# A cross-attention block on one core: the written-out front of the program in a new order, with 137 instead of 140 empty TensorE instructions

## The chip, the core and the metric

The kernel runs on one core of one Trainium2 chip. The core has five engines that work through queues of their own and wait for each other by semaphores: TensorE (PE in the profile, its weight loads PEld), VectorE (DVE), ScalarE (ACT), GpSimd (POOL) and SyncE (SP; SPq are the DMA issues of its queue). The metric is the device time of one execution in microseconds (us). Lower is better.

## The reference

A transformer block with cross-attention: 128 batches of 128 tokens, 256 features (D), 16 heads of 16 features, a feed-forward width of 1024, all float32. `query` is `x`, `key` and `values` are both `ctx`; `mask` is 0, so a token attends only to earlier ones and the first row of the attention is zero.

```python
q = (query @ Wq + bq).reshape(b, s, N_HEADS, D_K).transpose(0, 2, 1, 3)
k = (key @ Wk + bk).reshape(b, s, N_HEADS, D_K).transpose(0, 2, 1, 3)
v = (values @ Wv + bv).reshape(b, s, N_HEADS, D_K).transpose(0, 2, 1, 3)
scores = jnp.einsum('bhqd,bhkd->bhqk', q, k) / jnp.sqrt(jnp.float32(D_K))
...
allowed = j < i + mask
scores = jnp.where(allowed, scores, NEG_INF)
attn = jax.nn.softmax(scores, axis=-1)
if mask == 0:
    attn = attn.at[:, :, 0, :].set(0.0)
ctx = jnp.einsum('bhqk,bhkd->bhqd', attn, v)
...
attn_out = ctx @ Wo + bo
x = layer_norm(query + attn_out, ln1_g, ln1_b)
ffn = jax.nn.relu(x @ W1 + b1) @ W2 + b2
out = layer_norm(x + ffn, ln2_g, ln2_b)
```

## The kernel before

**Tiling.** Two batches are one pair `p`, 0 to 63. A pair goes through these stages: its tokens are loaded in 32x32 blocks (`load`, L92) and turned (`tokens`); queries, keys and values are projected; `scores` and `scores_both` (L440) multiply queries by keys into eight banks of PSUM; the mask, the maximum, the exponential and the sum follow; the attention is turned, `weigh` (L586) multiplies it by the values, `context` takes the product out of its bank, `attention_out` applies Wo, `attention_sum` adds the tokens; then come the first layer norm, the hidden layer (`hidden`), the second product (`second`) and the second norm. The scores of a pair fall into a high half (queries 64 to 127 of each batch, 128 keys a row) and a low half (queries 0 to 63, which need 64 keys).

**Order.** The kernel is written with a manual schedule: on each of the five engines the instructions stand in the order in which the Python statements issue them, and no scheduler moves any. So the place of a statement in the code is the place of all its instructions, on every engine it uses, the DMA issues included. Pairs 0 to 6 and steps 7 and 8 are written out one statement at a time; this is the front. A step `p` is not one pair: it has the scores of pair p, the weighing of pair p-2, the hidden layer of pair p-3, the second product of pair p-4 and the second norm of pair p-6. In steps 7 and 8 each statement is `do(key, p)`, with `key` from the table `OPS`. From step 9 on the loop `for p in range(9, 61): step(p)` takes its keys from one string, `ORDER`. Steps 61 to 63 are written out again. `empty(n)` puts n empty instructions into TensorE's queue.

**Softmax, two ways.** For pairs 0 to 4, `maximum` takes the maximum of a part on VectorE (L475) and subtracts it on GpSimd (L476), `exponential` is one wide ScalarE instruction, and `sums` takes the row sums and reciprocals on VectorE (L499) and scales the part on GpSimd (L500). From pair 5 on, `exponential_by_head` (L937) does one head at a time on ScalarE, with the maximum as bias and the sum as a by-product, and the reciprocals are applied later, when `context` reads the product. High-half heads are read from the PSUM banks, four heads to a bank, and free them; low-half heads are read from `sm` in SBUF, where `mask` put them. In steps 7 and up `eh0` to `eh7` are two high heads each, `el0` to `el7` two low heads each.

**Turning the attention.** Pairs 0 and 1 are turned on TensorE (`turn_on_pe`). From pair 2 on, `turn` transposes 32x32 blocks on VectorE from `sm` into the one buffer `turned` (L533), in three parts, and `bring` moves the blocks across partitions with 16 DMAs from `turned` to `brought` (L552), most of them issued by SyncE. `weigh` reads `brought`. Both buffers exist once, so pair p+1 can be turned only when the 16 transfers of pair p have read `turned`, and be brought only when pair p has been weighed.

**Mixed weights.** From step 7 on a 2x2 block product is done with seven products instead of eight (class `Seven`; `v1` to `v4`, `q1` to `q4`, `k1` to `k4`, `o1` to `o4`), and the same in the hidden layers of later pairs. For this GpSimd makes sums of weight blocks once (`combine_weights`, L1105 to L1108, four instructions for each of Wq, Wk, Wv and Wo; `combine_w1`, `combine_w2`) and sums of data blocks for every pair (`combine_x`, `combine_c`; `xc`, `cc`, `oc`, `hs`, `xs` in the steps). In a step, `v1`, `v2`, `v3`, `v4` write to one bank in turn, and `vk0`, `vk1`, `vk2`, `vr` are the ScalarE copies (`vr` is L1278) that empty it between them.

**Other names.** `add_bo` (L295, GpSimd) adds the output bias to the tokens of a pair. `residual1` (L721 and the line behind it, GpSimd) makes the input of the second sum. `deviation` and `shift` (GpSimd) make the scales of a norm. `load_ahead(p)` issues the block loads of later tokens: for an even p those of `x` of pairs p+4 and p+5, for an odd p those of `ctx` of pairs p+3 and p+4. `load_tokens(g)` loads the plain tokens of pairs 2g and 2g+1, `store(p)` writes a result. `tokens_ahead` is the same as `load_tokens` for the steps.

## Time and profile before

| | |
|---|---|
| time of three runs | 1468.98, 1472.11, 1474.38 us, median 1472.11 |
| the profiled execution | 1469.98 us, of which 1468.2 are its span |
| granted TensorE clock, mean over the span | 0.997 |
| HBM | 55.06 MB read, 18.09 MB written |
| front, up to the first weighing of step 9 | 184.8 us |
| loop, steps 9 to 60 | 52 rounds of about 22.0 us |

The profile counts an engine as busy while an instruction of it runs; register, branch, semaphore and DMA-issuing instructions do not count. In the timeline a row is a group of instructions of one line: start, length, engine, line, operation, output and input tile, count, and in brackets the idle time ahead of it and what ended it. The windows give for each stretch the busy time of each engine, the number of its instructions in brackets, the granted TensorE clock (1.00 is full), the busy share of the DMA engines and the GB/s that they moved. Times are counted from the start of the span. All names of pairs are cut from the tiles in the profile, so that the pair is known from the time and the order.

### The profile page before, as it was taken

What the parts mean: (1) busy time and instruction counts of PE and PEld (TensorE: products, weight loads), DVE (VectorE), ACT (ScalarE), POOL (GpSimd) and SP (SyncE); (2) the same over time, 40 slices, a digit from 0 to 9 for tenths busy, and PEclk for the clock granted to TensorE, in tenths of its full rate; (3) what the DMA queues carried; (4) which work ended last, traced back from release to release, by engine and by line L of the source; (5) the groups of instructions that cost most, each with busy time, mean ns of one, the idle gap of its engine ahead of it and who ended that gap; (6) DMA issues with size and microseconds to landing.
All of it is one profiled execution on the core that took longest, in us unless ns stands there. A gap on an engine that the chain in (4) does not pass through costs nothing.

```text
span 1468.2 us, 62017 instructions
## 1 busy us (share of the span) xinstructions
PE 1447.0 (99%) x20713; PEld 1391.6 (95%) x20713; DVE 1371.9 (93%) x3175; ACT 1303.4 (89%) x5559; POOL 1271.2 (87%) x1872
## 2 busy tenths in 40 slices
PE   8999899999999999999999999999999999999998
PEld 7778799999999999999999999999999999999988
DVE  6987999999999999999999999999999999999767
ACT  5659899999999999999999999999999999999743
POOL 5986898988988988988988998998998998998966
PEclk9999999999999999999999999999999999999999
DMA  8274766766766766766766766766766776774541
GB/s 208 63 143 102 179 154 156 162 157 156 161 160 153 162 158 153 163 160 153 160 158 157 159 158 158 160 158 156 163 157 153 163 161 149 164 158 116 140 103 51
DMA packets 367881, 220.34 MB, mean 150 GB/s; under 512 B 280032, under 2 KB 335584, under 8 KB 367584
## 3 DMA queue, kind: packets, MB, share of 16 engines
q1 hardware_dynamic: 365296, 214.27, 63.8%
q8 instruction: 187, 3.06, 1.0%
q10 hardware_dynamic: 2288, 2.11, 0.7%
q14 instruction: 110, 0.90, 0.2%
HBM read 55.06 MB, written 18.09 MB: 50 GB/s over the span
## 4 chain that ended last, share of the span: by engine, by line
PE 92%; DVE 4%; POOL 1%; DMA 1%; ACT 1%; issue 1%; SPq 0%; DVEq 0%; ACTq 0%; POOLq 0%
PE banks L1153 48%; PE banks L1364 24%; PE banks L440 6%; PE banks L596 4%; PE banks L586 2%; PE banks L300 2%; PE banks L875 2%; PE banks L977 1%; PE banks L635 1%; PE banks L356 1%; DVE sm L464 1%; ACT sm L937 1%; DVE turned L533 1%; PE banks L1050 0%; PE banks L1412 0%
## 5 line engine op out<-in xcount | busy, mean ns | idle before, releaser
L937 ACT ACTIVATE sm<-banks,nmx 128x128 f32<-128x128 f32 x944 | 340.8, 396 | 17.9 <-DVE nmx L1568 14.7
L937 ACT ACTIVATE sm<-sm,nmx 128x64 f32<-128x64 f32 x944 | 325.2, 384 | 1.5 <-DVE nmx L926 1.5
L937 ACT ACTIVATION_READ_ACCUMULATOR sm<-banks,nmx 128x1 f32 x944 | 222.8, 236 | 0.0
L937 ACT ACTIVATION_READ_ACCUMULATOR sm<-sm,nmx 128x1 f32 x944 | 221.8, 235 | 0.0
L533 DVE STREAM_TRANSPOSE turned<-sm 128x1024 f32<-128x1024 f32 x186 | 217.0, 1214 | 3.3 <-DMA brought<-turned 1.8
L1153 PE MATMUL banks<-wt,hS 128*128 128x128 f32 x1344 | 177.7, 275 | 0.0
L1364 PE MATMUL banks<-xS,w1t 128*128 128x128 f32 x1344 | 177.2, 275 | 0.0
L1153 PEld LDWEIGHTS banks<-wt,hS 128*128 128x128 f32 x1344 | 163.6, 192 | 0.1
L1364 PEld LDWEIGHTS banks<-xS,w1t 128*128 128x128 f32 x1344 | 163.4, 192 | 0.0
L1568 DVE TENSOR_REDUCE nmx<-banks 128x4 f32<-128x512 f32 x224 | 152.3, 680 | 1.9
L1557 POOL TENSOR_TENSOR hS<-hT 128x512 f32<-128x512 f32 x116 | 148.2, 1279 | 3.7 <-ACT hT L882 2.4
L1364 PE MATMUL banks<-brought,w 128*128 128x128 f32 x896 | 118.2, 275 | 0.0
L1153 PE MATMUL banks<-w,hT 128*128 128x128 f32 x896 | 109.8, 275 | 0.0
L1364 PEld LDWEIGHTS banks<-brought,w 128*128 128x128 f32 x896 | 109.0, 192 | 0.0
L1618 POOL TENSOR_TENSOR x1b<-x,g_r 128x512 f32<-128x512 f32 x56 | 72.4, 1293 | 39.4 <-ACT x L709 39.4
L1153 PEld LDWEIGHTS banks<-w,hT 128*128 128x128 f32 x896 | 104.8, 192 | 0.1
L440 PE MATMUL banks<-kT,qT 32*64 32x128 f32 (+1 forms) x3840 | 98.3, 331 | 1.8 <-ACT vz L1278 1.5
L1393 ACT ACTIVATE hT<-hT,b1e_c 128x256 f32<-128x256 f32 x224 | 95.7, 510 | 1.2 <-DVE hT L1389 1.1
L1562 DVE TENSOR_TENSOR banks<-banks,neg 128x256 f32<-128x256 f32 x224 | 93.3, 417 | 0.0
L440 PEld LDWEIGHTS banks<-kT,qT 32*64 32x64 f32 x3840 | 79.4, 131 | 12.6 <-ACT vz L1278 1.9
L709 ACT ACTIVATE x<-t,nb,sd 128x256 f32<-128x256 f32 x126 | 68.4, 593 | 19.7 <-POOL nb L732 12.9
L1219 ACT ACTIVATE kr<-banks,b_c 128x128 f32<-128x128 f32 x224 | 83.7, 411 | 1.7 <-PE banks L1153 1.7
(324 smaller groups left out, 4821.5 us busy)
## 6 DMA issues: line engine op xcount, KB each, us to landing
brought<-turned SPq DMA_DIRECT2D x936, 128.0 KB, 2.4
out_dram<-t SPq DMA_DIRECT2D x63, 256.0 KB, 4.0
xb<-in_x_dram SPq DMA_DIRECT2D x124, 128.0 KB, 3.2
cb<-in_ctx_dram SPq DMA_DIRECT2D x124, 128.0 KB, 3.2
x<-in_x_dram SPq DMA_DIRECT2D x56, 256.0 KB, 2.8
kT<-kr SPq DMA_DIRECT2D x112, 128.0 KB, 2.2
brought<-turned SPq DMA_DIRECT2D x40, 96.0 KB, 2.4
w<-in_L_xattn_W_dram SPq DMA_DIRECT2D x2, 1024.0 KB, 7.4
```

What stands on the lines that cost most here:

```text
L440: nc.tensor.matmul(st["sps", hi][r][s * HP : (s + 1) * HP, m * 2 * n : (m + 1) * 2 * n].rearrange("p (e j) -> p e j", e=2), st["qT"][strip ...
L533: nc.vector.transpose(turned[:, :, at : at + 256].rearrange("p j (n a) -> p n j a", a=32), states[p]["sm", hi].rearrange("p h j -> p (h j) ...
L709: nc.scalar.activation(x1[:, s], t1[:, s], AF.Identity, bias=st["nb", 1][:, s], scale=sd[:, s])
L937: nc.scalar.activation(sm[:, h, :], src, AF.Exp, bias=nmx[:, h : h + 1], scale=1.0, **({"accum_out": st["su"][:, at : at + 1]} if summed e ...
L1153: nc.tensor.matmul(out, left(k) if self.depth > 1 else left, right(k) if self.depth > 1 else right, start=(n == 1 and k == 0), stop=(k == ...
L1219: nc.scalar.activation(self.k[:, m, s * P : (s + 1) * P], src, AF.Identity, bias=bk_c[:, m : m + 1], scale=1.0,)
L1364: nc.tensor.matmul(ps[:, i * P : (i + 1) * P].rearrange("p (n a) -> p n a", a=32), left(i), right, start=(n in (1, 2, 5) and i == 0), stop ...
L1393: nc.scalar.activation(self.hT[:, f, at], self.hT[:, f, at] if src is None else src, AF.Relu, bias=b1e_c[:, f : f + 1], scale=1.0,)
L1557: engine.tensor_tensor(c[:, n], left, right, how)
L1562: nc.vector.tensor_tensor(ps[:, :, HP:], ps[:, :, HP:], neg[:, 1, None, :].to_broadcast([P, 4, HP]), ALU.add)
L1568: nc.vector.tensor_reduce(states[p]["nmx", 1][:, 4 * b : 4 * b + 4], banks[:, b].rearrange("p (n j) -> p n j", j=P), AX.X, ALU.max, negate ...
L1618: nc.gpsimd.tensor_tensor(st["x1b"], st["x1b"] if n else st["x1"], (be1b_r if n else g1_r)[:, None, :].to_broadcast([P, 2, D]), ALU.add if ...
```

## The change

The statements between `states[3]["x1T"] = x1_view(3)` and the loop stand in a new order. The same statements are called with the same arguments; the counts of instructions on VectorE, ScalarE, GpSimd and SyncE stay as they were, and TensorE has 137 empty instructions between the products of steps 7 and 8 where it had 140 (27 groups of five and one of two, for 28 groups of five). Nothing ahead of the front and nothing from step 9 on is touched. Two calls that were split by others now stand together (`second(0, 0)` with `second(0, 1)`, and the same for pair 1), and the halves of `bring(2, ...)` are issued in the other order.

The diff, cut to where statements move past many others. First the start and pairs 0 to 2, with `combine_weights` of all four weights:

```diff
     states[3]["x1T"] = x1_view(3)
     tokens(2, "x")
+    combine_weights(wv, wvt)
+    combine_weights(wo, wot)
     scores(0, 1)
     mask(0, 1, A)
...
+    hidden(0, range(0, 2), None, (2, 3, 4, 0))
+    hidden(0, range(2, 4), None, (2, 3, 4, 0))
+    combine_weights(wq, wqt)
+    turn_on_pe(1, 1, range(3, 4))
...
+    sums(2, 0, ALL)
+    combine_weights(wk, wkt)
+    add_bo(3)
+    turn(2, 1, 1)
+    context(1)
+    project_keys(3)
+    turn(2, 1, 0)
+    attention_out(1)
+    load_ahead(2)
+    turn(2, 0, 0)
     tokens(4, "c")
...
+    load_ahead(3)
     copy_keys(3)
```

Pairs 2 to 4, with the loads, the transfers of pair 2 and `add_bo(4)`:

```diff
-    bring(2, nc.sync, EVERY[:8])
-    context(1)
-    residual1(0)
-    scores(3, 1)
-    mask(3, 1, B)
-    bring(2, nc.scalar, EVERY[8:])
...
+    residual1(0)
+    bring(2, nc.scalar, EVERY[8:])
     hidden(0, range(6, 8), None, (2, 3, 4, 0))
...
+    exponential(3, 1, TWO)
+    bring(2, nc.sync, EVERY[:8])
+    weigh(2)
...
+    load_ahead(4)
+    nc.gpsimd.tensor_tensor(b1e_c, b1e_c, b1_c, ALU.add)
+    load_ahead(5)
...
-    load_ahead(2)
-    load_ahead(4)
...
-    add_bo(4)
-    tokens(6, "x")
-    combine_w1()
...
-    load_ahead(3)
-    copy_keys(5)
-    copy_queries(5)
-    load_ahead(5)
...
+    load_tokens(2)
     attention_out(3)
...
-    combine_weights(wk, wkt)
...
-    combine_weights(wo, wot)
...
+    store(0)
+    bring_all(5, EVERY[0:4])
...
-    combine_weights(wq, wqt)
...
+    add_bo(4)
     attention_sum(4)
...
-    combine_weights(wv, wvt)
```

Step 7 up to the scores of step 8. Before, in its last part:

```diff
-    do("v4", 7)
-    do("stats1", 7)
-    do("means", 7)
-    do("turn1", 7)
-    do("k4", 7)
-    do("q4", 7)
-    do("kr", 7)
-    do("eh0", 7)
-    do("qr", 7)
-    do("weigh", 8)
-    do("eh1", 7)
...
-    do("context", 8)
-    do("oc0", 8)
-    do("el4", 7)
-    do("el3", 7)
-    do("ks2", 7)
-    do("el7", 7)
-    do("turn2", 7)
-    do("vr", 7)
-    do("scores", 8)
-    do("maskA0", 8)
```

And in the change:

```diff
+    do("eh1", 7)
+    do("tokc", 7)
+    do("vr", 7)
+    do("br1", 7)
+    do("weigh", 8)
+    do("turn1", 7)
+    do("ks", 7)
+    do("hs0", 7)
     do("hs1", 7)
+    do("eh0", 7)
+    do("means", 7)
+    do("eh2", 7)
+    do("el3", 7)
     do("hs2", 7)
...
+    do("context", 8)
+    do("el1", 7)
+    do("xs2", 7)
+    do("hs3", 7)
+    do("ks2", 7)
+    do("scores", 8)
     do("turn0", 7)
+    do("add3", 8)
+    do("max3", 8)
+    do("el2", 7)
+    do("el6", 7)
```

And the empty instructions, where the products of steps 7 and 8 stand between each other:

```diff
+    do("w1", 7)
+    do("w5", 7)
+    empty(2)
     do("q1", 8)
     empty(5)
+    do("v2", 8)
+    empty(5)
...
     do("o1", 8)
     empty(5)
-    do("w1", 7)
...
-    do("w5", 7)
-    empty(5)
-    do("add1", 8)
```

More of the change, by code (lines that the diff above doesn't have):

```diff
@@ L2151, in tile_cross_attention_block @@
     exponential_by_head(6, 0, range(8, 12), True)
[L2152 to L2155 removed]
     second_half(2, 1)
+    turn_x1_blocks(4)
+    do("weigh", 7)
+    do("context", 7)
     exponential_by_head(6, 0, range(0, 4), True)
[L2158 to L2160 removed]
+    copy_keys(7)
+    do("res0", 7)
+    do("oc2", 7)
+    hidden(3, range(2, 4), None, (2, 3, 4, 6))
+    load_ahead(6)
+    turn(6, 1, 1)
```

733 lines of the change are left out of this document (356 added, 377 removed).

## The prediction

> **What bounds the kernel now.** I read the page first, then the chain of waits, then the busy time by stage, and then the timelines of single engines at the stage borders.
>
> ```profile
> span 1468.2 us, 62017 instructions
> PE 1447.0 (99%) x20713; PEld 1391.6 (95%) x20713; DVE 1371.9 (93%) x3175; ACT 1303.4 (89%) x5559; POOL 1271.2 (87%) x1872
> ```
>
> TensorE (PE) is nearly always busy, so time is saved only where it waits. The chain of waits shows the loop behind the front (columns: start, length, what):
>
> ```profile
> 188.10 8.24 PE banks L1153 x72
> ...
> 210.06 8.24 PE banks L1153 x72
> ...
> 232.03 8.23 PE banks L1153 x72
> ```
>
> The same piece returns after 21.96 and 21.97 us. The loop `step(9)` to `step(60)` is the same code in both kernels, so its 52 rounds cost the same, and the change acts on the 184.8 us ahead of it. This table cuts the front at its stage borders; the last row is one loop round (columns: stretch, its length, busy us of PE, weight loads, VectorE, ScalarE, GpSimd, then clock and DMA).
>
> ```profile
> 23.00:62.20 39.20, 38.68 (x527) 30.89 (x526) 35.91 (x54) 32.57 (x65) 36.70 (x26) 1.00 0.34 77
> 62.20:84.20 22.00, 21.61 (x218) 18.45 (x217) 21.27 (x36) 10.61 (x19) 20.81 (x19) 1.00 0.75 162
> 84.20:104.50 20.30, 20.30 (x240) 17.41 (x239) 17.43 (x24) 9.73 (x21) 18.07 (x13) 1.00 0.71 150
> 104.50:125.50 21.00, 19.58 (x237) 15.60 (x235) 17.35 (x32) 18.61 (x85) 9.78 (x19) 1.00 0.43 97
> 125.50:146.80 21.30, 21.30 (x246) 17.98 (x246) 16.66 (x29) 19.77 (x86) 16.25 (x26) 1.00 0.57 119
> 146.80:163.00 16.20, 11.43 (x218) 9.74 (x217) 13.77 (x35) 14.54 (x79) 11.45 (x20) 1.00 0.67 159
> 163.00:184.80 21.80, 21.19 (x235) 20.55 (x235) 21.30 (x50) 19.52 (x88) 19.78 (x32) 1.00 0.81 193
> 206.80:228.80 22.00, 22.00 (x331) 21.56 (x329) 21.34 (x52) 20.88 (x93) 19.68 (x30) 1.00 0.70 158
> ```
>
> PE's idle time from 23 us to the loop is 0.52 + 0.39 + 0 + 1.42 + 0 + 4.77 + 0.61 = 7.7 us. That is the ceiling for any new order of the same PE work, apart from short waits inside busy rows. It is 0.52% of the time, and 0.5% (7.4 us) is about what a measurement of this kernel can tell from no change. So "faster" needs nearly all of it. From 20 to 82 us GpSimd is as full as PE (36.70 of 39.20, 20.81 of 22.00): whatever is added to its queue there delays the softmax of the first pairs.
>
> **The change, part by part.** No instruction is added or removed except three empty ones, so the cost lies in which wait ends last. Two places carry the sum.
>
> First place: GpSimd. These are its rows around the scaling of pair 2 (L500, `sm_2`), before; L476 `sm_3` is the next pair's subtraction:
>
> ```order
> L500 TENSOR_TENSOR sm_2_705<-sm_2_705,rs1_2_8_862 128x1024
> L500 TENSOR_TENSOR sm_2_705<-sm_2_705,rs1_2_0_873 128x1024
> L500 TENSOR_TENSOR sm_2_705<-sm_2_705,rs0_2_0_910 128x1024
> L295 TENSOR_TENSOR x_1_140<-x_1_140,bov_r_182 128x512
> L721 TENSOR_TENSOR x1b_0_998<-x1_0_727,g1_r_134 128x512
> ```
>
> And in the change, at the same place in the program:
>
> ```order
> L1105 TENSOR_TENSOR wqt_190<-wq_86 128x128
> L1106 TENSOR_TENSOR wqt_190<-wq_86,wqt_190 128x128
> L1107 TENSOR_TENSOR wqt_190<-wq_86 128x128
> L1108 TENSOR_TENSOR wqt_190<-wq_86,wqt_190 128x128
> L500 TENSOR_TENSOR sm_2_708<-sm_2_708,rs1_2_8_945 128x1024
> L500 TENSOR_TENSOR sm_2_708<-sm_2_708,rs1_2_0_950 128x1024
> L500 TENSOR_TENSOR sm_2_708<-sm_2_708,rs0_2_0_962 128x1024
> L1105 TENSOR_TENSOR wkt_191<-wk_85 128x128
> L1106 TENSOR_TENSOR wkt_191<-wk_85,wkt_191 128x128
> L1107 TENSOR_TENSOR wkt_191<-wk_85 128x128
> L1108 TENSOR_TENSOR wkt_191<-wk_85,wkt_191 128x128
> ```
>
> The mixes of Wq and Wk, which stood behind pair 5, now stand on both sides of pair 2's scaling. Up to the scaling of pair 3 nothing leaves this queue in exchange: the four `add_bo`, both residuals, `be1b_r` and the deviations are the same sets.
>
> ```profile
> 6.62 0.37 SPq L107 DMA_DIRECT2D wo<-in_L_xattn_Wo_dram  x1
> ...
> 19.99 5.61 POOL L476 TENSOR_TENSOR sm<-sm,nmx 128x1024 f32<-128x1024 f32 x3 [14.86 <-DVE nmx L475]
> ...
> 76.11 5.62 POOL L500 TENSOR_TENSOR sm<-sm,rs 128x1024 f32<-128x1024 f32 x3
> ...
> 83.28 1.28 POOL L295 TENSOR_TENSOR x<-x,bov_r 128x512 f32<-128x512 f32 x1
> ...
> 91.69 5.61 POOL L476 TENSOR_TENSOR sm<-sm,nmx 128x1024 f32<-128x1024 f32 x3 [2.08 <-DVE nmx L475]
> 97.26 5.62 POOL L500 TENSOR_TENSOR sm<-sm,rs 128x1024 f32<-128x1024 f32 x3
> ...
> 119.01 0.46 POOL L1105 TENSOR_TENSOR wkt<-wk 128x128 f32<-128x128 f32 x1
> ...
> 120.79 0.47 POOL L1105 TENSOR_TENSOR wot<-wo 128x128 f32<-128x128 f32 x1
> ```
>
> One mix takes 120.79 - 119.01 = 1.78 us, two take 3.56. The scaling of pair 3, which ends at 76.11 + 5.62 = 81.73, should end at 85.3. The mixes of Wv and Wo go to the head of the queue, into the 14.86 us in which GpSimd waits for the first maximum: 3.6 us that cost nothing here and no longer stand in the way later. If their weights landed too late, the whole softmax would move with them; the later of the two loads is issued by SyncE (SPq) at 6.62, over 13 us ahead of 19.99, so I take zero. Pair 4's `add_bo` (1.28) moves behind its softmax, so that pair's GpSimd work gets back part: 3.56 - 1.28 = 2.3 later, less the 2.08 us it waits for VectorE at 91.69, hence about 0.2, up to 2 if that wait stays.
>
> What pair 3 delays is a chain of transposes and transfers through one buffer, `turned`. VectorE turns a pair into it, SyncE issues 16 transfers, and only when those have read it can the next pair be turned:
>
> ```profile
> 80.64 3.50 DVE L533 STREAM_TRANSPOSE turned<-sm 128x1024 f32<-128x1024 f32 x3 [0.22 <-issue]
> ...
> 101.05 3.50 DVE L533 STREAM_TRANSPOSE turned<-sm 128x1024 f32<-128x1024 f32 x3 [0.62 <-POOL sm L500]
> ...
> 117.99 2.37 DVE L533 STREAM_TRANSPOSE turned<-sm 128x1024 f32<-128x1024 f32 x2 [1.77 <-DMA brought<-turned]
> 121.00 1.25 DVE L533 STREAM_TRANSPOSE turned<-sm 128x1024 f32<-128x1024 f32 x1 [0.64 <-ACT sm L937]
> ```
>
> ```profile
> 84.20 1.83 SPq L552 DMA_DIRECT2D brought<-turned  x3
> ...
> 92.36 5.66 SPq L552 DMA_DIRECT2D brought<-turned  x9
> 98.05 7.38 SPq L92 DMA_DIRECT2D cb<-in_ctx_dram  x8
> ...
> 123.71 10.89 SPq L552 DMA_DIRECT2D brought<-turned  x16
> ...
> brought<-turned SPq DMA_DIRECT2D x936, 128.0 KB, 2.4
> ```
>
> Pair 3's last transfer is issued at 92.36 + 5.66 = 98.0 and lands 2.4 later, at 100.4. With 3.56 more it lands at 104.0, which is later than the 101.05 at which pair 4 is turned now. From there: two turns at 1.15, a sum and statistics that now stand between (about 1.3), the last turn 1.15, so the transfers of pair 4 start near 108.6. Before, they waited behind eight context loads until 105.4 (98.05 + 7.38), loads which the change issues before pair 2's transfers; so the difference is 3.1 us. Pair 5's turn, at 117.99 released by pair 4's transfers, goes to 121.1; it needn't wait again for ScalarE (0.64 at 121.00), so its transfers start about 2.4 later, at 126.1, and land at 126.1 + 10.9 + 2.4 = 139.4. Pair 5's weighing waits for them:
>
> ```profile
> 138.19 0.43 PE L586 MATMUL banks<-brought,vd 128*32 128x64 f32 x16
> ...
> 146.77 1.71 PE L440 MATMUL banks<-kT,qT 32*64 32x128 f32 x64
> ...
> 160.18 0.55 PE L586 MATMUL banks<-brought,vd 128*32 128x64 f32 x16 [1.43 <-ACT qT L1181]
> ...
> 163.00 1.60 PE L440 MATMUL banks<-kT,qT 32*64 32x128 f32 x64 [1.15 <-ACT vz L1278]
> ```
>
> It moves from 138.2 to 139.4, and step 7's scores behind it from 146.8 to 148.0. **Term 1: +1.2 us** (from 0, if the chain's slack is larger, to +3.6, if nothing absorbs it).
>
> Second place: ScalarE in step 7. Before, its rows ahead of step 8's scores (64-wide rows are low-half exponentials `el`, 128-wide ones from `banks` the high half; L1278 frees the bank of the values):
>
> ```order
> L937 ACTIVATE sm_7_2193,su_7_2260<-banks_184,nmx1_7_2195 128x128 x2
> L1181 ACTIVATE qT_8_2264<-banks_184,bqs_c_243 128x128
> L937 ACTIVATE sm_7_2193,su_7_2260<-banks_184,nmx1_7_2195 128x128 x2
> L937 ACTIVATE sm_7_2193,su_7_2260<-sm_7_2193,nmx0_7_2194 128x64 x6
> L1278 COPY vz1_178<-banks_184 128x4x2x16
> ```
>
> And in the change:
>
> ```order
> L937 ACTIVATE sm_7_2217,su_7_2259<-banks_184,nmx1_7_2219 128x128 x2
> L1278 COPY vz1_178<-banks_184 128x4x2x16
> L937 ACTIVATE sm_7_2217,su_7_2259<-banks_184,nmx1_7_2219 128x128 x4
> L937 ACTIVATE sm_7_2217,su_7_2259<-sm_7_2217,nmx0_7_2218 128x64 x8
> L937 ACTIVATE sm_8_2446,su_8_2490<-banks_184,nmx1_8_2448 128x128 x2
> ```
>
> L1278 has moved ahead, and eight low heads, which hold no bank, stand behind all that the next scores need.
>
> ```profile
> 161.58 0.46 ACT L937 ACTIVATE sm<-sm,nmx 128x64 f32<-128x64 f32 x1
> ...
> 162.25 0.45 ACT L937 ACTIVATE sm<-sm,nmx 128x64 f32<-128x64 f32 x1
> ```
>
> Two heads take 162.25 - 161.58 = 0.67, eight take 2.7 us. ScalarE was busy 14.54 of 16.20 in that stage and its vz copy ended PE's last wait, so the scores of step 8 can come up to 2.7 us sooner after those of step 7. What is late next is VectorE: from 146.8 to 184.8 it is busy 13.77 + 21.30 = 35.07 of 38.0 us, and in a loop round 21.34 of 22.00 (0.97). At that density the two steps take 35.07 / 0.97 = 36.2. **Term 2: -1.8 us** (from 0, if the eight heads are missed in step 8, where ScalarE has only 2.3 us idle, to -2.7).
>
> The rest I cost at nothing. The three empty instructions: four pairs of matmuls with five empties behind them take no longer than the eight matmuls do,
>
> ```profile
> 172.20 1.06 PE L1153 MATMUL banks<-w,hS 128*128 128x128 f32 x8
> 173.09 0.39 PE L1153 MATMUL banks<-xc,wqt 128*128 128x128 f32 x2
> ```
>
> The next row starts 173.09 - 172.20 = 0.89 us later, 0.11 for each of the eight, and the loop's rows above have 8.24 / 72 = 0.11. The loads asked for earlier lie in SyncE's idle time before pair 2's transfers; `load_tokens(2)` and `store(0)` each put one issue (about 0.5) ahead of a pair's transfers, part of the 0 to +3.6. The ScalarE transfers of pair 2 keep their place behind the turn of pair 2.
>
> Sum: 1.2 - 1.8 = -0.6. The profiled execution took 1469.98 (span 1468.2), so the same execution would take 1469.4; the median of the runs, 1472.11, stands 2.13 above it, which gives **1471.5**.
>
> [...] The granted clock falls once, after PE waited for the first masks:
>
> ```profile
> 16.00:20.00 4.00, 2.44 (x34) 1.46 (x35) 4.00 (x7) 1.13 (x4) 0.01 (x1) 0.95 0.95 202
> 20.00:24.00 4.00, 4.00 (x13) 3.27 (x12) 3.96 (x7) 1.90 (x3) 4.00 (x3) 0.63 0.83 277
> ```
>
> At 0.63 over 4 us PE loses 1.5 us. The wait stays, since the same masks follow the same load, so I leave the loss as it is. [...]
>
> **The rivals.** (a) The freed waits: the new order lets PE run through, and all 7.7 us of idle go: 1472.1 - 7.7 = 1464.4. For it: step 7 alone holds 4.8 of them. Against: GpSimd and VectorE are full at the same time in the first 60 us, and VectorE again in step 8. (b) The chain of `turned` ends slower: pair 3's 3.56 us passes from turn to turn without being absorbed, and step 7's gain is lost because pair 7's transfers, whose turns now wait for the eight low heads, come too late for the loop's first weighing. Price: +3.6 and 0, so 1475.7; it decides once pair 5's transfers land over 1.3 us after the 138.2 of now. Twice that, +7.4 and more, would need a second buffer wait of the same size. (c) The clock: one half-rate stretch more or less, 1470.0 or 1473.0, inside the forecast.
>
> **How the numbers follow.** Forecast, -4 to +3 us around the sum: 0.60. (a), -4 to -8: 0.20, with 0.10 of it beyond 7.4. (b), +3 to +7: 0.14. Beyond on either side: 0.02 faster, 0.04 slower. So faster by over 0.5% 0.12, within 0.5% 0.82, slower 0.06. The range takes in (b)'s 1475.7 and (a)'s 1464.4 with a little beyond: 1463.5 to 1477.0.
>
> **What would show it.** Right: the scaling of pair 3 (L500) ends near 85 us instead of 81.7, pair 4's turn is released by a transfer rather than by GpSimd, step 7's scores start at 147 to 149, and step 8's scores follow 14 us later instead of 16.2. Wrong: if GpSimd ends pair 3 before 83 us, term 1 is gone and (a) gains; if PE waits at the loop's first weighing for a transfer, (b) is at work.

## The result and the profile after

The changed kernel is slower: a median of 1483.13 us (1480.96 to 1484.16, six runs) against 1470.53 us (1468.98 to 1474.38, six runs) for the kernel before on the same chip. The ratio is 1.0080, with a 95% interval of 1.0067 to 1.0094. The profiled execution of the changed kernel took 1480.96 us, the lowest of its six; that of the kernel before took 1469.98, so the two profiles below are 10.98 us apart.

These are two parts of the page of the changed kernel: busy time by engine, and two pieces of the chain of waits (start, length, what).

```profile
span 1479.2 us, 62006 instructions
PE 1448.8 (98%) x20713; PEld 1392.1 (94%) x20713; DVE 1374.8 (93%) x3175; ACT 1303.1 (88%) x5559; POOL 1270.1 (86%) x1872
...
197.95 8.23 PE banks L1153 x72
...
219.92 8.23 PE banks L1153 x72
```

The work is the same and the loop's round is the same (219.92 - 197.95 = 21.97), but the loop's first piece starts at 197.95 instead of 188.10, that is 9.85 us later. Step 60's scores stand 10.06 later (1316.93 against 1306.87), so the loop adds 0.2; the last 0.9 of the 10.98 arise behind it and weren't looked into.

Busy time by stage shows where the 9.85 us arise. Columns: stretch, its length, busy us of PE, weight loads, VectorE, ScalarE and GpSimd, then clock and DMA. The borders are the same events in both kernels: the end of pair 2's scaling (L500), the end of pair 3's scaling, the scores of step 7 (L440), those of step 8, and the first weighing of step 9 (L586). Before:

```profile
60.84:81.73 20.89, 20.50 (x233) 17.16 (x218) 20.22 (x35) 9.76 (x17) 19.89 (x17) 1.00 0.72 160
81.73:146.77 65.04, 63.62 (x722) 53.14 (x720) 53.85 (x86) 49.16 (x191) 46.35 (x61) 1.00 0.57 121
...
146.77:163.00 16.23, 11.46 (x218) 9.77 (x217) 13.77 (x35) 14.56 (x80) 11.48 (x20) 1.00 0.67 159
```

The fourth row of before, 163.00 to 184.80, stands in the prediction. After:

```profile
61.02:86.44 25.42, 23.97 (x252) 18.85 (x251) 24.19 (x40) 10.79 (x21) 23.47 (x22) 1.00 0.57 123
86.44:151.63 65.19, 60.87 (x714) 51.82 (x712) 52.41 (x80) 50.43 (x192) 41.39 (x50) 1.00 0.53 122
151.63:167.28 15.65, 11.72 (x218) 9.91 (x217) 11.88 (x28) 12.50 (x65) 9.04 (x14) 1.00 0.55 130
167.28:194.64 27.36, 23.44 (x233) 22.39 (x233) 23.68 (x57) 22.48 (x104) 22.10 (x36) 0.94 0.63 154
```

Up to pair 2's scaling the change costs 0.18, then the four stages cost +4.53, +0.15, -0.58 and +5.56, together 9.84. **Two places lose most of it.** The 0.18 is flattered by the clock: in its first 100 us the execution of before lost 1.7 us to half clock (the 0.63 in the prediction's row from 20 us), that of the change nothing, so apart from the clock the change is about 1.9 later there too. The run vr_ahead (below), which has the order of before through step 7's scores and lost nothing to half clock ahead of them, agrees: pair 2's scaling ends at 59.10 in it, 1.92 sooner than in the change, and step 7's scores start at 145.02, 6.6 sooner. So the first part costs 4.9 us by the two profiles and 6.6 clock apart.

The second row is worth a look. TensorE waits 65.19 - 60.87 = 4.3 us in it, against 1.4 before, and yet it keeps its length, because TensorE has 2.75 us less to do in it (60.87 against 63.62; in the stretch ahead it did 3.47 more). From pair 3's scaling to pair 5's scores it takes 22.6 instead of 24.2, and from these to step 7's scores 42.6 instead of 40.8. What the new order saves in the one part comes back as waits in the other: one behind pair 5's scores (1.10 before) and one at the weighing of pair 4, for its transfers (none before). These are TensorE's rows of them, after (start, length, what; in brackets the idle time before it and what ended it):

```profile
113.44 1.78 PE L300 MATMUL banks<-cT,wk 128*128 128x256 f32 x7 [2.81 <-ACT sm L937]
...
123.22 0.43 PE L586 MATMUL banks<-brought,vd 128*32 128x64 f32 x16 [0.89 <-DMA brought<-turned]
```

So step 7 is late by about as much as pair 3's scaling. But TensorE itself loses most of it behind that scaling: of the 5.8 us that it waits between pair 2's scaling and step 7's scores (1.8 before), 4.3 lie behind pair 3's scaling.

**First place: pair 3's softmax.** GpSimd in the changed kernel, the columns as in the row above:

```profile
60.98 0.46 POOL L1105 TENSOR_TENSOR wkt<-wk 128x128 f32<-128x128 f32 x1
...
69.63 5.66 POOL L476 TENSOR_TENSOR sm<-sm,nmx 128x1024 f32<-128x1024 f32 x3
...
79.45 1.90 POOL L500 TENSOR_TENSOR sm<-sm,rs 128x1024 f32<-128x1024 f32 x1 [1.32 <-DVE rs L499]
81.31 1.27 POOL L295 TENSOR_TENSOR x<-x,bov_r 128x512 f32<-128x512 f32 x1
...
82.69 3.75 POOL L500 TENSOR_TENSOR sm<-sm,rs 128x1024 f32<-128x1024 f32 x2
```

The mix of Wk does stand in the way (1.78 us from 60.98), but behind it GpSimd waits 1.32 us for the reciprocal (L499) of VectorE. Behind that wait `add_bo(2)` and a short row (81.31 to 82.69) stand between the first and the other two scalings of pair 3, 1.4 us in which GpSimd has no idle time; before, the three follow each other (the row at 76.11 in the prediction). VectorE is busy 24.19 of the 25.42 us. In its timeline, after:

```profile
62.22 0.67 DVE L289 STREAM_TRANSPOSE cT<-cb 128x512 f32<-128x512 f32 x1
...
65.30 0.70 DVE L289 STREAM_TRANSPOSE cT<-cb 128x512 f32<-128x512 f32 x1
...
72.51 2.93 DVE L713 TENSOR_SCALAR x<-t,mv,sd 128x256 f32<-128x256 f32 x2
...
79.10 0.20 DVE L499 RECIPROCAL rs<-su 128x8 f32<-128x8 f32 x1
```

The two L289 rows are `tokens(4, "c")` and `tokens(5, "c")`, which the change puts ahead of pair 3's sums; `stats(0, states[0]["t2"], 2)` (four instructions from 76.79, 1.2 us) is a third. In all 2.6 us. And L713 (`norm1`) takes 2.93 us here; before, it took

```profile
69.91 1.46 DVE L713 TENSOR_SCALAR x<-t,mv,sd 128x256 f32<-128x256 f32 x2
```

**Second place: the scores and values of step 8.** TensorE, before and then after:

```profile
164.68 0.71 PE L1153 MATMUL banks<-wv,cT 128*128 128x128 f32 x4
```

```profile
172.31 0.71 PE L1153 MATMUL banks<-wv,cT 128*128 128x128 f32 x4 [3.15 <-DVE sm L464]
```

The values of step 8 (`v1`) wait 3.15 us for a mask of VectorE on `sm`. This is VectorE's timeline ahead of that mask, after:

```profile
168.35 1.24 DVE L533 STREAM_TRANSPOSE turned<-sm 128x1024 f32<-128x1024 f32 x1
169.51 0.40 DVE L1562 TENSOR_TENSOR banks<-banks,neg 128x256 f32<-128x256 f32 x1
169.95 0.69 DVE L1568 TENSOR_REDUCE nmx<-banks 128x4 f32<-128x512 f32 x1
170.56 1.23 DVE L533 STREAM_TRANSPOSE turned<-sm 128x1024 f32<-128x1024 f32 x1
171.83 0.42 DVE L464 TENSOR_TENSOR sm<-banks,neg 128x256 f32<-128x256 f32 x1
```

`sm` holds the low half of the scores, and there is one copy of it. Step 8's first low mask (L464 at 171.83) writes it, so it can run only when the last turn of step 7 (`turn2`, L533 at 170.56) has read it, and that turn needs the low heads' exponentials. In the changed order eight of those stand behind step 8's scores on ScalarE, and `turn0`, `add3` and `max3` (168.35 to 170.64) stand ahead of `turn2` on VectorE.

The wait has a sequel. TensorE's clock in stretches of 2 us, after (same columns as above):

```profile
172.00:174.00 2.00, 1.69 (x12) 1.70 (x13) 1.15 (x3) 2.00 (x7) 1.72 (x3) 0.84 0.00 0
174.00:176.00 2.00, 2.00 (x11) 2.00 (x11) 1.93 (x5) 1.78 (x6) 1.02 (x1) 0.50 0.01 4
176.00:178.00 2.00, 2.00 (x17) 2.00 (x16) 2.00 (x5) 0.63 (x3) 0.00 (x0) 0.81 0.64 145
```

TensorE lost 2 x (0.16 + 0.50 + 0.19) = 1.7 us, which is 3.4 us at half clock. So of TensorE's time in the fourth stage's +5.56, 3.3 are waits (3.92 us of idle PE against 0.61, and 3.15 of them this one), 1.7 the clock, and 0.55 other time of a busy PE. But the half clock isn't what makes the stage long. Two of the runs below, vector_light and mid_old, have the same statements from step 7's scores on and the same wait of 3.15, and no half clock falls into the stage. It is as long, 27.44 and 27.30 us:

```profile
171.07:198.51 27.44, 22.08 (x232) 20.83 (x233) 23.45 (x57) 22.65 (x104) 22.89 (x36) 1.00 0.63 154
```

```profile
168.70:196.00 27.30, 22.11 (x232) 20.83 (x232) 23.41 (x57) 22.69 (x104) 22.95 (x36) 1.00 0.63 154
```

TensorE waits there instead: 1.44 and 1.28 us for VectorE's L1383 shortly ahead of step 9's weighing, where the change waits 0.33.

### The profile page after: what moved, and what is told of

Its sections match the earlier page's. It is cut to its first block, busy times and chain, and to the rows that moved or that the text cites. A ratio compares the mean times of both kernels' runs of the same rounds, so it can differ in the third digit from the quotient of the medians.

```text
span 1479.2 us, 62006 instructions
## 1 busy us (share of the span) xinstructions
PE 1448.8 (98%) x20713; PEld 1392.1 (94%) x20713; DVE 1374.8 (93%) x3175; ACT 1303.1 (88%) x5559; POOL 1270.1 (86%) x1872
## 4 chain that ended last, share of the span: by engine, by line
PE 89%; DVE 4%; SPq 3%; DMA 1%; POOL 1%; ACT 1%; issue 1%; DVEq 0%; POOLq 0%; ACTq 0%
PE banks L1153 48%; PE banks L1364 23%; PE banks L440 6%; PE banks L596 4%; PE banks L586 2%; PE banks L875 2%; SPq L92 1%; PE banks L977 1%; SPq L552 1%; DVE sm L464 1%; PE banks L300 0%; DMA brought<-turned 0%; DVE nmx L475 0%; PE banks L894 0%; PE banks L1412 0%
## 5 line engine op out<-in xcount | busy, mean ns | idle before, releaser
L533 DVE STREAM_TRANSPOSE turned<-sm 128x1024 f32<-128x1024 f32 x186 | 217.4, 1214 | 3.2 <-POOL sm L500 1.1
L937 ACT ACTIVATION_READ_ACCUMULATOR sm<-banks,nmx 128x1 f32 x944 | 218.4, 231 | 0.0
L937 ACT ACTIVATION_READ_ACCUMULATOR sm<-sm,nmx 128x1 f32 x944 | 215.5, 228 | 0.0
L1618 POOL TENSOR_TENSOR x1b<-x,g_r 128x512 f32<-128x512 f32 x56 | 72.4, 1293 | 40.8 <-ACT x L709 40.8
L440 PE MATMUL banks<-kT,qT 32*64 32x128 f32 (+1 forms) x3840 | 97.6, 331 | 1.2 <-DMA kT<-kr 0.9
L440 PEld LDWEIGHTS banks<-kT,qT 32*64 32x64 f32 x3840 | 79.6, 131 | 10.9 <-ACT sm L937 1.0
```

The lines of the kernel that those rows point to most:

```text
L440: nc.tensor.matmul(st["sps", hi][r][s * HP : (s + 1) * HP, m * 2 * n : (m + 1) * 2 * n].rearrange("p (e j) -> p e j", e=2), st["qT"][strip ...
L533: nc.vector.transpose(turned[:, :, at : at + 256].rearrange("p j (n a) -> p n j a", a=32), states[p]["sm", hi].rearrange("p h j -> p (h j) ...
L937: nc.scalar.activation(sm[:, h, :], src, AF.Exp, bias=nmx[:, h : h + 1], scale=1.0, **({"accum_out": st["su"][:, at : at + 1]} if summed e ...
L1618: nc.gpsimd.tensor_tensor(st["x1b"], st["x1b"] if n else st["x1"], (be1b_r if n else g1_r)[:, None, :].to_broadcast([P, 2, D]), ALU.add if ...
```

## The experiments

All kernels compute the same thing in another order. The table holds medians (the kernel before in the same set of runs in brackets), the ratio with its 95% interval, and five stretches of each profile in us: from pair 0's to pair 2's scaling, from there to pair 3's, on to the scores of step 7, from these to the scores of step 8, and from step 7's scores to step 9's first weighing. The last column is what TensorE's clock lacked, in us, summed over 2 us stretches: up to 100 us, and from 100 to 200.

| kernel | median | ratio | 0-2 | 2-3 | 3-s7 | s7-s8 | s7-w9 | clock lack |
|---|---|---|---|---|---|---|---|---|
| before | 1470.53 | - | 29.4 | 20.9 | 65.0 | 16.2 | 38.0 | 1.7+0 |
| after | 1483.13 (1470.53) | 1.0080 [1.0067, 1.0094] | 31.1 | 25.4 | 65.2 | 15.6 | 43.0 | 0+1.7 |
| tail_new | 1476.48 (1469.95) | 1.0036 [1.0022, 1.0050] | 29.7 | 20.9 | 65.0 | 14.9 | 43.2 | 1.7+1.7 |
| head_new | 1479.91 (1469.95) | 1.0059 [1.0038, 1.0080] | 30.9 | 25.5 | 65.8 | 16.2 | 38.0 | 1.7+1.7 |
| mixes_back | 1482.81 (1469.95) | 1.0083 [1.0063, 1.0102] | 30.6 | 25.5 | 65.5 | 15.6 | 44.0 | 3.4+5.1 |
| start_new | 1471.24 (1469.95) | 1.0005 [0.9995, 1.0015] | 28.5 | 20.9 | 65.0 | 16.2 | 38.1 | 1.7+0 |
| early_old | 1482.98 (1471.34) | 1.0090 [1.0065, 1.0115] | 34.5 | 25.5 | 64.5 | 15.6 | 43.4 | 6.8+1.7 |
| vr_ahead | 1469.68 (1471.34) | 0.9993 [0.9982, 1.0005] | 28.4 | 20.9 | 65.0 | 15.5 | 38.1 | 0+0 |
| queries_first | 1482.75 (1471.34) | 1.0086 [1.0064, 1.0109] | 30.9 | 25.4 | 64.9 | 15.6 | 43.5 | 1.7+1.7 |
| pair1_first | 1485.97 (1471.34) | 1.0104 [1.0084, 1.0125] | 33.5 | 25.5 | 65.8 | 15.6 | 43.9 | 3.4+5.1 |
| vector_light | 1485.46 (1470.24) | 1.0106 [1.0089, 1.0123] | 31.9 | 24.2 | 67.5 | 15.6 | 43.0 | 1.7+1.7 |
| mask_first | 1484.62 (1470.24) | 1.0098 [1.0083, 1.0113] | 30.9 | 25.4 | 64.1 | 15.6 | 43.6 | 1.7+3.4 |
| mask_bo5 | 1484.46 (1470.24) | 1.0101 [1.0086, 1.0116] | 31.3 | 25.5 | 65.5 | 14.9 | 42.8 | 1.7+1.7 |
| all_three | 1485.05 (1470.24) | 1.0103 [1.0088, 1.0118] | 30.9 | 24.2 | 68.6 | 14.9 | 42.2 | 1.7+5.1 |
| mixes_early | 1473.30 (1471.07) | 1.0017 [1.0007, 1.0026] | 29.9 | 22.7 | 65.0 | 16.2 | 38.0 | 0+0 |
| vector_heavy | 1473.36 (1471.07) | 1.0013 [1.0004, 1.0023] | 28.4 | 24.0 | 65.9 | 16.2 | 39.0 | 1.7+3.4 |
| both_early | 1473.87 (1471.07) | 1.0018 [1.0007, 1.0028] | 30.9 | 23.9 | 64.3 | 16.2 | 38.0 | 1.7+0 |
| mid_old | 1481.69 (1471.07) | 1.0064 [1.0046, 1.0081] | 29.4 | 20.9 | 71.7 | 15.6 | 42.9 | 1.7+1.7 |

### The two halves alone

**tail_new**: the order of before through step 7's scores, then the order of the change.

```diff
     do("scores", 7)
-    turn(6, 1, 0)
-    reciprocals(6)
...
+    combine_c(7)
+    store(0)
...
```

> The order of before up to and with the scores of step 7, then the order of the change for all that is left. Theory: steps 7 and 8 lose about 5 us by themselves (the low heads that now stand behind the scores of step 8 hold sm, so that step 8's first mask and the values behind it wait): 1475.5 us, and step 9's first weighing about 190 us instead of 184.8. Rival 1, as recorded: the new steps 7 and 8 gain 1.8 us by themselves, 1468.7. Rival 2: they lose only because the first part comes late, so 1470.5.

Measured: 6.5 us slower than before, and the wait of the changed kernel at the same instruction, to the hundredth:

```profile
166.50 1.22 PE L1153 MATMUL banks<-wv,cT 128*128 128x128 f32 x4 [3.15 <-DVE sm L464]
```

Step 8's scores come 1.3 us sooner behind step 7's (14.9 instead of 16.2), as term 2 said; then step 9's weighing comes 5.2 us later behind step 7's scores (43.2 against 38.0). The gain exists and is overpaid within the next step.

**head_new**: the other half, the change's order through step 7's scores and then that of before.

```diff
     do("scores", 7)
+    add_bo(5)
+    do("br0", 7)
     do("maskA0", 7)
-    do("v1", 7)
-    do("vk0", 7)
...
```

> The order of the change up to and with the scores of step 7, then the order of before for all that is left. Theory: the first part costs 4.9 us (step 7's scores at 151.7 instead of 146.8), so 1475.4 us. Rival: nearly all of the 12.6 us comes from the first part and steps 7 and 8 only pass it on: 1481 or more.

Measured: 10.0 us slower, between the two expectations. The stage up to pair 3's scaling is as long as in the changed kernel (25.5), and the second half is that of before (38.0). Its profile and tail_new's lack 3.4 us of clock, those of before and after 1.7 each. Step 9's weighing is 8.0 later than before in head_new and 4.9 in tail_new. If the excess of 1.7 is lost in full, which isn't shown, 6.3 and 3.2 are left; together 9.5, near the 9.84 of the change. In either case each half has a loss of its own.

### The first place: GpSimd's mixes or VectorE's queue?

**start_new**: only the first stretch of the change, through `scores(1, 1)`, on the order of before. It holds the mixes of Wv and Wo at the head of GpSimd's queue.

```diff
     tokens(2, "x")
+    combine_weights(wv, wvt)
+    combine_weights(wo, wot)
     scores(0, 1)
...
-    combine_weights(wo, wot)
...
-    combine_weights(wv, wvt)
```

> The order of the change only up to the first scores of pair 1, then the order of before. Theory: TensorE's waits ahead of 20 us fall from 5.1 to 1.6 us and the first subtraction on GpSimd comes 1.9 us earlier, and as GpSimd is full from there, 1.9 to 3.5 us are kept: 1467.0 to 1468.6. Rival: it is given back in pairs 1 to 3, where VectorE is as full: 1470.5.

Measured: the same as before, so the 1.9 to 3.5 us that I expected to gain aren't there. The prediction's zero for the mixes of Wv and Wo holds.

**early_old**: the reverse, the changed kernel with the order of before through `scores(2, 1)`.

```diff
     tokens(2, "x")
-    combine_weights(wv, wvt)
-    combine_weights(wo, wot)
     scores(0, 1)
     mask(0, 1, A)
-    values(0)
...
+    mask(0, 1, B)
```

> The order of before up to and with the first scores of pair 2, then the order of the change. Theory: of the loss of the first part about 4 us stand ahead of 60 us (turns of pairs 0 and 1 on TensorE wait for scalings that stand behind other work on VectorE and GpSimd), so 1479 us. Rival: what comes later (pair 3's chain, the scores of pair 5, step 8) sets the time anyway and the change's 1483 stays.

Measured: no gain (1.0090), the rival's case, and pair 2 to pair 3 still takes 25.5. That loss arises behind `scores(2, 1)`.

**mixes_back**: the changed kernel with the mixes of Wq and Wk behind `residual1(3)`, where they don't stand ahead of pair 3.

```diff
-    combine_weights(wq, wqt)
     turn_on_pe(1, 1, range(3, 4))
...
-    combine_weights(wk, wkt)
     add_bo(3)
...
     residual1(3)
+    combine_weights(wq, wqt)
+    combine_weights(wk, wkt)
```

> The change with the mixes of Wq and Wk behind the third residual, where GpSimd has idle time, instead of around pair 2's scaling. Recorded theory: pair 3's scaling ends 3.56 us earlier on GpSimd and the whole chain of transposes and transfers follows: 1479.6 us. Rival: in the change VectorE and the weights of the scores set that chain, GpSimd only waits more, and the time stays within 1 us of the change's 1483.1.

Measured: no change, which was the rival's. Without the mixes GpSimd waits for VectorE all the same:

```profile
82.44 1.90 POOL L500 TENSOR_TENSOR sm<-sm,rs 128x1024 f32<-128x1024 f32 x1 [1.29 <-DVE rs L499]
```

The cause that the prediction named for term 1 isn't what limits the changed kernel there.

**queries_first** and **pair1_first**: two guesses at other parts of the new order, pair 5's low mask and the queries of pair 6 taken up sooner, and pair 1's low half finished sooner.

```diff
     scores_both(5)
+    mask(5, 0, A)
+    project_queries(6)
     norm2(0)
...
-    mask(5, 0, A)
-    project_queries(6)
```

```diff
     mask(1, 0, A)
+    maximum(1, 0, ALL)
     scores(2, 1)
     sums(1, 1, TWO)
+    exponential(1, 0, ALL)
+    sums(1, 0, ALL)
...
-    maximum(1, 0, ALL)
...
-    exponential(1, 0, ALL)
-    sums(1, 0, ALL)
```

> The change, but behind the scores of pair 5 TensorE goes on with the queries of pair 6 (they need one low mask), as before, instead of the keys of pair 6 (they need a high mask and four heads of ScalarE). Theory: TensorE's wait there falls from 2.8 to about 1.4 us and no half clock follows it, 1480 to 1481.5 us. Rival: pair 4's transfers, issued from 110.1 us, set the next weighing, the wait moves there, 1483.

> The change, but the low half of pair 1 is finished (maximum, exponential, sum) ahead of pair 2's masks and maxima, as before. Theory: GpSimd's last scaling of pair 1 comes about 4 us sooner and TensorE's wait of 1.7 to 2 us ahead of pair 1's turns goes, 1481 us. Rival: pair 2 comes as much later and the time stays at 1483.

Measured: queries_first changes nothing that can be told, and pair1_first is no help (1.0104, with the stretch to pair 2 at 33.5). Both guesses fall. In queries_first the rival's reason is seen: the wait behind pair 5's scores falls from 2.81 to 1.60, and the one for pair 4's transfers rises from 0.89 to 1.85.

```profile
124.87 0.43 PE L586 MATMUL banks<-brought,vd 128*32 128x64 f32 x16 [1.85 <-DMA brought<-turned]
```

So the chain through `turned` that the prediction followed does hold TensorE in the new order, at pair 4's weighing and not at pair 5's.

What makes pair 2's scaling 1.9 late in the change, clock apart, stays open. The first stretch of its order doesn't (start_new), and without the mix of Wq, in mixes_back, the stretch to pair 2 is hardly shorter (30.6 instead of 31.1).

**vector_light**: the changed kernel with VectorE's three tasks taken away from where they precede pair 3's sums, and two loads that wait for them moved too.

```diff
     sums(2, 1, ONE)
+    tokens(4, "c")
...
-    tokens(4, "c")
-    load_ahead(3)
...
-    tokens(5, "c")
...
-    stats(0, states[0]["t2"], 2)
...
+    tokens(5, "c")
...
+    stats(0, states[0]["t2"], 2)
```

> The change with three pieces of VectorE work moved out of the stretch between pair 2's and pair 3's scaling, to about where they stood before: the turn of pair 4's context tokens (0.67 us) ahead, the turn of pair 5's context tokens (0.70) and the statistics of pair 0's second norm (1.25) behind; the two loads that wait for those tokens go with them. Theory: VectorE sets that stretch (25.4 us in every kernel with the change's order there, with the mixes or without, 20.9 before), it shrinks by 2.6 to 22.8, and the time falls to about 1480.4 us. Rival: GpSimd or TensorE takes over and it stays at 1483.

Measured: pair 2 to pair 3 shrinks by 1.2 (24.2), half of what was expected, and the time doesn't shrink: the following stretch grows to 67.5, with 1.7 us lost to half clock in it (116 to 120 us), where the change lost none. GpSimd no longer waits for the reciprocal (its scaling at 80.95 has no idle time before it), so in that stretch GpSimd takes over, as the rival said. What each part is worth can't be read from the changed kernel, because the next wait takes over. So the next three go the other way and add the parts to the kernel before.

**mixes_early**: only the mixes of Wq and Wk, moved as in the change. **vector_heavy**: only VectorE's three tasks. **both_early**: both.

```diff
     maximum(2, 0, ALL)
+    combine_weights(wq, wqt)
     sums(2, 1, TWO)
...
     sums(2, 0, ALL)
+    combine_weights(wk, wkt)
...
-    combine_weights(wk, wkt)
...
-    combine_weights(wq, wqt)
```

```diff
-    tokens(4, "c")
...
     turn(2, 0, 0)
+    tokens(4, "c")
...
     mask(3, 1, B)
+    tokens(5, "c")
...
     second_sum(0)
+    stats(0, states[0]["t2"], 2)
...
-    tokens(5, "c")
...
-    stats(0, states[0]["t2"], 2)
```

> The kernel before with the mixes of Wq and Wk around pair 2's scaling, as in the change, and nothing else. Recorded theory with the chain passing all of it: GpSimd is full there, pair 3's scaling ends 3.56 us later and all of step 7 with it, 1473.8 us. Rival: VectorE sets pair 3's scaling, 1470 to 1471.

> The kernel before with three pieces of VectorE work where the change has them, ahead of pair 3's sums: the turns of the context tokens of pairs 4 and 5 (0.67 and 0.70 us) and the statistics of pair 0's second norm (1.25). Theory: pair 3's scaling ends 2.6 us later and step 7's scores with it, 1472.8 us. Rival: GpSimd sets pair 3's scaling and VectorE has room, 1470 to 1471.

> mixes_early and vector_heavy together. Theory: VectorE and GpSimd work in turns on pair 3 (mask and maximum, subtraction, sum, scaling), so both delays count, in part side by side: pair 3's scaling 4 to 6 us later, 1474 to 1476 us. Rival: they lie beside each other and only the longer counts, 1473.8 or less.

Measured, by the stretch from pair 2 to pair 3 (20.9 before): mixes_early 22.7, which is the 1.78 of one mix, that of Wk; vector_heavy 24.0, or 3.1 for tasks of 2.6; both 23.9, the longer of the two and not their sum. GpSimd and VectorE take turns at one pair, so a delay on one hides behind the other's.

The mix of Wq stands ahead of that stretch, and its cost shows in the one before: 1.5 us from pair 0's scaling to pair 2's, if profiles are compared that lost as much to half clock in their first 100 us (mixes_early 29.9 against 28.4 in vr_ahead, which lost nothing; both_early 30.9 against 29.4 in before, 1.7 each). So the two mixes make pair 3's scaling 3.3 us late in mixes_early, near the 3.56 of the prediction, and mixes and tasks together make it 4.5 late in both_early, which is the 4 to 6 that was expected.

The scaling of pair 3 in mixes_early and vector_heavy:

```profile
77.91 5.61 POOL L500 TENSOR_TENSOR sm<-sm,rs 128x1024 f32<-128x1024 f32 x3
```

```profile
76.36 5.61 POOL L500 TENSOR_TENSOR sm<-sm,rs 128x1024 f32<-128x1024 f32 x3 [1.30 <-DVE rs L499]
```

The wait of 1.30 comes with VectorE's tasks, not with the mixes, and it is the 1.32 of the changed kernel. In mixes_early the stretch behind stays at 65.0, as in before, start_new, vr_ahead and tail_new: nothing of the delay is absorbed. TensorE's rows show why. It loses the time at once, ahead of pair 3's scaling: its wait for VectorE's sum L904 grows from 0.38 in vr_ahead to 2.42, and there is a new one of 0.98 for L683 (at 64.57).

```profile
72.91 1.99 PE L300 MATMUL banks<-cT,wk 128*128 128x256 f32 x8 [0.38 <-DVE t L904]
```

```profile
76.46 1.99 PE L300 MATMUL banks<-cT,wk 128*128 128x256 f32 x8 [2.42 <-DVE t L904]
```

These are 3.0 of the 3.3 us, and a TensorE that is busy 63.62 of 65.04 us in the stretch behind (in before) can't make them up. In both_early that stretch is 64.3, so 0.7 of 4.5 is absorbed. By the medians mixes_early and vector_heavy are where their theories put them (1473.30 for 1473.8, 1473.36 for 1472.8), both_early (1473.87) lies between its theory and its rival. Each of the three is 2.2 to 2.8 us slower than before; by the time alone they can't be told from each other.

Of the change's 25.4 both_early explains 23.9. The other 1.5 us are as much as `add_bo(2)` and the row behind it (1.4 us), which stand between pair 3's scalings in every run that takes 25.4 or 25.5 there and in none of these three; this is read from the rows and wasn't tried by itself. L713's lengthening is not the reason: both_early has it in part (2.00 us), and in the runs that take 25.4 or 25.5 it is anything from 2.31 (mixes_back) to 2.93 (the change).

### The second place: the one copy of `sm`

**vr_ahead**: the kernel before with `vr` of step 7 (L1278) ahead of the last six low heads (three statements): the idea of term 2 alone, without the rest.

```diff
     do("oc0", 8)
+    do("vr", 7)
     do("el4", 7)
     do("el3", 7)
...
     do("el7", 7)
     do("turn2", 7)
-    do("vr", 7)
     do("scores", 8)
```

> The kernel before with one statement moved: the last copy of step 7's values, vr, stands ahead of the last six low heads of step 7. This is my recorded term for step 7 alone. Recorded: TensorE's wait for that copy (1.15 us) goes and step 8 comes sooner, 1468.2 to 1468.9 us. Theory now: step 8's first mask writes the one sm, so it waits for the turn of those low heads; TensorE's wait moves behind the scores, to the values of step 8, with the same end, and the time stays at 1470.

Measured: the same as before. TensorE's rows show why:

```profile
160.48 1.59 PE L440 MATMUL banks<-kT,qT 32*64 32x128 f32 x64 [0.38 <-DMA kT<-kr]
163.06 0.71 PE L1153 MATMUL banks<-wv,cT 128*128 128x128 f32 x4 [0.99 <-DVE sm L464]
```

The scores come 0.8 sooner behind step 7's (their wait was 1.15, for L1278, and is 0.38), and the values behind them wait 0.99 for the low mask, where before had no wait; step 9's weighing comes 38.1 us behind step 7's scores, as before (38.0). The gain of term 2 is taken back one row later, by `sm`, even in the mildest form.

**mask_first**: the changed kernel with `add3` and `max3` of step 8 behind the low mask. **mask_bo5**: the same, and `add_bo(5)` sooner. **all_three**: mask_bo5 and vector_light.

```diff
     do("turn0", 7)
-    do("add3", 8)
-    do("max3", 8)
     do("el2", 7)
     do("el6", 7)
     do("turn2", 7)
     do("maskA0", 8)
+    do("add3", 8)
+    do("max3", 8)
```

```diff
     add_bo(4)
+    add_bo(5)
...
     do("br0", 7)
-    add_bo(5)
```

> The change with the high mask and maximum of step 8 (add3, max3) behind its first low mask instead of ahead of the last turn of step 7. Theory: the turn and the mask come about 1 us sooner, TensorE's wait ahead of step 8's values falls from 3.15 to about 2.2 us, and if no half clock follows it, 2.6 us are saved: 1480.5 us; 1482 with the half clock. Rival: the eight low heads on ScalarE end step 7 and the later high maximum costs as much, 1483.

> As mask_first, and the output bias of pair 5 (1.27 us on GpSimd), which the change put between the first and the second mix of step 7's context, back among GpSimd's idle time behind that of pair 4. Theory: the keys of step 7 no longer wait for it, the scores of step 8 come up to 1.2 us sooner after those of step 7 (15.65 now), 1.2 us less than mask_first. Rival: the low heads on ScalarE set the end of step 7, no difference to mask_first.

> vector_light and mask_bo5 together. Theory: the three add up, about 1476.5 to 1478 us. Rival: what one place gains, the next takes back, 1480 or more.

Measured: the wait falls from 3.15 to 2.42, about as expected,

```profile
172.10 1.22 PE L1153 MATMUL banks<-wv,cT 128*128 128x128 f32 x4 [2.42 <-DVE sm L464]
```

and add_bo(5) shortens step 7 by 0.7 (14.9). None of the three is faster than the change. In mask_first's profile half clock lasts 6.8 us around the end of this wait, where it was 3.4 behind it in the change, and the stage is longer, 28.0 us. But all_three, with the wait of 2.42 and half clock for 3.4 us as in the change, takes 27.3 as well: what is saved at the values is waited one row later, for the second low mask (L456).

```profile
176.52 2.08 PE L1153 MATMUL banks<-w,hT 128*128 128x128 f32 x8 [0.73 <-DVE sm L456]
```

So the stage isn't set by this one mask. TensorE and VectorE wait for each other in it (in the change VectorE also waits 1.24 us for TensorE, ahead of its row at 188.88), and the first low mask is what TensorE meets first. What sets the stage's length stays open. No run puts the eight low heads alone back ahead of step 8's scores. That they are the cause, and not another move of this half, is argued from the rows and from vr_ahead, and not shown.

**mid_old**: the changed kernel with the order of before through `scores_both(4)`, and all that this leaves over, four mixes among it, put behind it.

```diff
     scores_both(4)
+    combine_weights(wv, wvt)
+    combine_weights(wo, wot)
+    combine_weights(wq, wqt)
+    combine_weights(wk, wkt)
...
     mask(4, 0, A)
```

> The order of before up to and with the scores of pair 4, then the order of the change. Theory: step 7's scores come 65 us after pair 3's scaling in either order, so the first part costs nothing here, and the time is that of tail_new, 1476.5 us. Rival: pairs 4 to 6 in the change's order cost time of their own (TensorE waits 2.8 us behind pair 5's scores): 1479 or more.

Measured: pair 2 to pair 3 is back at 20.9, but the next stretch takes 71.7. My four mixes (7.1 us) fell ahead of pair 4's subtraction on GpSimd and made a new delay. The run tells nothing between the theories.

## Why the prediction was wrong

The forecast was 1471.5 with a range to 1477.0; the median is 1483.13. By the profiles: the front up to pair 3 and on to step 7's scores was to cost 1.2 and cost 4.9 (146.77 to 151.63); steps 7 and 8 were to gain 1.8 and lost 5.0 (38.0 to 43.0). Those two misses, 3.7 and 6.8, are 10.5 of the 11.6 by which the sum missed the profiled 1480.96. The rest of the working held: the loop, the three empties, and the mixes of Wv and Wo at nothing (start_new, 1.0005).

**Term 1, the amount.** I took 3.56 us on GpSimd as the delay of pair 3 and predicted an end at 85.3. In the order of before that is nearly what the mixes cost: mixes_early has 3.3. But the changed kernel ended pair 3 at 86.44 for another reason, since taking the mixes away frees nothing there (mixes_back). The step that failed is the list of what stands ahead of pair 3. I worked it through for GpSimd, on the ground that GpSimd was as full as PE, and not for VectorE, which was busy 21.27 of 22.00 in the same row that I quoted; vector_heavy shows VectorE's tasks to be worth 3.1 in that stretch. And on GpSimd I counted sets ("the four `add_bo` ... are the same sets") and not places: `add_bo(2)` moved from ahead of pair 3's subtraction to between its scalings, behind the wait for VectorE.

**Term 1, the passing on.** "Pair 5's weighing waits for them" was false in the row itself: the weighing at 138.19 has no idle time before it. I had taken the transfers' landing for its start. Going on from there I let the chain absorb 3.56 us down to 1.2, and that is the other half of the step that failed: mixes_early, which has the mixes and nothing else, absorbs nothing. TensorE, which the prediction called nearly always busy, has lost the time before the chain through `turned` comes into play. SyncE's rows after:

```profile
54.59 12.64 SPq L92 DMA_DIRECT2D cb<-in_ctx_dram  x4
67.41 5.11 SPq L552 DMA_DIRECT2D brought<-turned  x8
...
110.14 11.19 SPq L552 DMA_DIRECT2D brought<-turned  x16
...
128.33 10.72 SPq L552 DMA_DIRECT2D brought<-turned  x16
...
175.46 11.30 SPq L552 DMA_DIRECT2D brought<-turned  x16
```

Pair 5's transfers start 4.6 us later than before (128.33 against 123.71; I said 126.1), and the weighing comes at 143.05, 4.9 later (I said 139.4). Of pair 4 I wrote that its GpSimd work would be about 0.2 later, since GpSimd waited 2.08 for VectorE there and could use that up. But the wait stayed, because VectorE was late itself, and pair 4's scaling ended at 107.36 (its rows start at 101.75 and take 5.61) instead of 102.88. The upper bound of the term, +3.6 "if nothing absorbs it", was the right case; for the mixes alone it was the right amount too, and for the whole change too small. Pair 4's turn was released by a transfer, as forecast.

The first row above also refutes "the loads asked for earlier lie in SyncE's idle time". Four context loads hold SyncE's queue from 54.59 to 67.2 (four of them take 3.1 to 4.1 us elsewhere in the change's front), and pair 2's transfers start at 67.41. They seem to wait for the buffers that `tokens(4, "c")` and `tokens(5, "c")` read until 66.0. What that costs by itself wasn't tried; pair 2's weighing, at 74.30, has no wait before it.

**Term 2.** ScalarE's part was right: eight low heads behind the scores let them come sooner (15.65 instead of 16.23; 14.9 in tail_new). "What is late next is VectorE" was right about the engine and wrong about the way. I priced it by VectorE's density over two steps, 36.2 us, as if its work could lie anywhere. What I missed is the order in its queue: the low masks of step 8 write the one copy of `sm` and must wait for the last turn of step 7. tail_new has the loss with the first half untouched, and vr_ahead has the swap of 0.8 gained for 0.99 waited in miniature. Rival (b) named the turns that wait for the eight heads, but looked for the damage at the loop's first weighing, through pair 7's transfers. They do start 9.4 later (175.46 against 166.10), and nobody waits for them: issued by 186.8, landed 2.4 later, they are needed at 194.64.

**The clock.** Rival (c) took one half-rate stretch more or less (before has one, at 0.50 from 19.6 to 23.0 us) as equally likely and kept it inside the forecast; that was an estimate, and what brings such a stretch isn't shown. It wasn't symmetric. The change makes waits of 1.90, 2.81 and 3.15 us behind 25 us, where the longest before is 1.43. Every profile that has step 7 in the changed order lacks 1.7 us or more from 100 to 200 us; of the seven that have it in the order of before, five lack nothing there. But not all of what the clock lacks is paid: vector_light and mid_old lack nothing in step 8, and step 8 is as long in them. The change's profile is its lowest run, and its median lies 2.2 above; that the other runs drew one stretch more is argued from the table and not shown, since they have no profile.

No kernel here beats both: vr_ahead (0.9993) and start_new (1.0005) can't be told from the kernel before.

## What to carry to other kernels

When an order is rewritten, list what moves ahead of a critical piece on every engine that is full in that stage, not on the fullest alone: where two full engines took turns at one buffer, the longer delay counted (22.7 and 24.0 us alone, 23.9 together), and what a full TensorE had lost in waits was hardly made up behind them (nothing of 3.3 us in mixes_early, 0.7 of 4.5 in both_early). For each reader that is moved back, ask which instruction of the next round writes the same buffer and who waits for that; a buffer with one copy turned "later and off the path" into a wait one row further on (0.99 us in vr_ahead, 3.15 in the change). To find a cost in a tight kernel, add the suspect to the fast kernel: taken out of the slow one, it was masked by the next wait (1.29 us in mixes_back, 1.32 in the change). And look for its cost in every stretch that it touches, between profiles that lost as much to the clock.
